# Layer 1 of a Perceiver kernel: memories loaded as layer 0 turned them, instead of turned a second time

## The chip, the cores and the metric

The kernel runs on one core of a Trainium2 chip, in float32. The metric is the device time of one launch in microseconds (us). Before the change it is 1710.55 us, the median of three runs from 1708.24 to 1710.9.

## What is computed

Two layers work on a latent array x of 16 batches x 64 rows x 256. Both read the same context memory, ctx_1024, of 16 batches x 1601 rows x 256. Layer 0 has a cross-attention that keeps the 32 best scores of a row, a retention step and a block of attention and experts. Layer 1 has the cross-attention that this change is about, a random-feature step and a tree of small networks. The part that matters, cut from the reference:

```python
x = x + L0_xattn(layernorm(x), ctx_1024, 32, ...)      # q k v; scores; top 32; softmax; weigh
x = x + L0_attn(layernorm(x), ...)                     # retention
x = x + L0_ffn(layernorm(x), ...)                      # attention, then experts
x = x + L1_xattn(layernorm(x), ctx_1024, ctx_1024, ...)

def L1_xattn(q, k, v, norm_w, norm_b, ..., Wq, bq, Wk, bk, Wv, bv, Wo, bo):   # H = 16 heads of 16
    qn, kn, vn = (layernorm(t, norm_w, norm_b) for t in (q, k, v))
    Q, K, V = (qn @ Wq + bq, kn @ Wk + bk, vn @ Wv + bv)                      # split into heads
    A = softmax(Q K^T / 4)
    O = A V + Q
    return layernorm(O, norm1_w, norm1_b) @ Wo + bo + O
```

Here layernorm(t, w, b) is (t - mean) * rsqrt(var + eps) * w + b over the 256 columns. In layer 1 it is applied to every row of every memory, while layer 0 uses the memories as they are.

## The kernel before

A memory is a tile of 128 partitions x 13 chunks x 256: row c * 128 + p stands in chunk c of partition p, and chunk 12 has 65 rows. `load_mem` (L213) brings one with two DMAs on SyncE's queue, 1536 KB (L215) and 65 KB (L218). TensorE contracts over partitions, so both layers need a memory turned, with its 256 columns on the partitions: a tile mT of 128 x 2 x 1601.

The code is traced by a framework that places the waits. By default a planner orders each engine's instructions, by program order and by when it estimates that each can start. Inside a `tc.manual_schedule(engines=...)` block the engines named keep the order of the program. [...]

**Layer 0** (L225 to L394) takes the memories in 8 pairs. `turned_pair(k)` (L237) loads the pair (six memory buffers, so three pairs), turns it on TensorE (L248, 52 transposes) and copies the result from PSUM with ScalarE (L253) into two mT buffers. `scored_pair(k)` (L284) makes the scores from mT (L290), `choose` (L302) takes the 32 best of each row with VectorE (L312, L316, L322), and `gather(k - 2)` (L325) turns the weights (L333) and weighs the unturned memories (L346). The loop at L370 runs gather(k - 2) in steps between the 16 steps of turned_pair(k), then scores pair k. No engine is in written-out order here. A pair's memory buffers come free when its gather ends.

**Between the layers** stand retention, attention and experts (L515 to L896). Layer 1's weights w_x (`load_square`, L92, on GpSimd's queue) and its work on the first memories, traced at L899 to L910, are filled in there by the planner: three memories are loaded and normalised (`fetch`, L504), two are turned, and keys and values of memory 0 are made.

**Layer 1's loop** (L1096 to L1151) runs over 128 units: 16 batches b, 4 parts of the 1601 rows (PARTS: 512, 384, 384 and 321 rows), 2 halves oc of the columns (8 heads each). TensorE, VectorE and ScalarE are in written-out order. A unit u does, in this order: `score` (four matmuls groups, L981); a step of `keys` for batch b + 1 (L460, L468); for four groups of heads the maximum on VectorE (L995) and the exponential on ScalarE (L997), with a step of `keys` between; `turn_over` of the unit before (L1010, L1015, L1017); a step of `values` for batch b + 1 (L482, L490); in units 1 to 3 of a batch a step of `collect` for the batch before; in units 3 to 7 steps of `normalise`; a step of `turned_mem`; `weigh` of the unit before (L1029, L1036); a second step of `values`.

- `normalise` (L408, for memory b + 3): 13 times statistics of a chunk on VectorE (L415, L416); then the square root on ScalarE (L419), a reciprocal (L421), and 13 times the normalising of a chunk in place on GpSimd (L426). Four steps a unit, and what is left in unit 7.
- `turned_mem` (L432, for memory b + 2): 8 steps, each 3 or 4 transposes on TensorE (L439) and one ScalarE copy (L444) that also applies norm_w and norm_b.
- `collect` (L1041): joins the four parts of a batch. GpSimd computes wt (L1049) and tot (L1051) in unit 1, with an exponential on ScalarE between (L1050); VectorE makes parts (L1068) in units 2 and 3; GpSimd adds them up in unit 3 (L1076, L1080, L1084) and writes by_head to DRAM (L1085).

So memory b + 3 is loaded at the start of batch b, normalised during it, turned in the next batch, projected to keys and values in the one after, and scored in the one after that.

Of the kernel before, what the change touches and what calls it, by code (L numbers as in the profile page):

```python
# [9 lines left out]
F32 = mybir.dt.float32  # L10
# [8 lines left out]
B = 16  # L19
# [13 lines left out]
TURN_STEPS = ((3, 0), (3, 1), (1, 0), (1, 1), (2, 0), (2, 1), (0, 0), (0, 1))  # L33
# [32 lines left out]
def perceiver_kernel(  # L66
# [24 lines left out]

    def load_square(pool, src, n, name):  # L92
        t = pool.tile([P, n, 2, D], F32, name=name, tag=name)
        nc.gpsimd.dma_start(
            out=t.rearrange("p n c o -> p (n c) o"),
            in_=src.rearrange("(m p) o -> p m o", p=P),
        )
        return t
# [124 lines left out]


    with ExitStack() as ph:  # L225
# [11 lines left out]
        def turned_pair(k, mems, memTs):  # L237

            for h in range(2):
                mems.append(load_mem(memp, 2 * k + h))  # L240
                memTs.append(work.tile([P, 2, S], F32, name="mT", tag="mT"))
            for n0, n in SCH:
                for h in range(2):
                    for dc in range(2):
                        pt = ps_m.tile([P, 512], F32, name="pt", tag="mm")
                        for j in range((n + P - 1) // P):
                            c = n0 // P + j
                            nc.tensor.transpose(  # L248
                                pt[:, j * P : j * P + chunk(c)],
                                mems[h][0 : chunk(c), c, dc * P : (dc + 1) * P],  # L250
                                ident[0 : chunk(c), 0 : chunk(c)],
                            )
                        nc.scalar.copy(memTs[h][:, dc, n0 : n0 + n], pt[:, 0:n])  # L253
                        yield

        first_mems, first_memTs = [], []
        for _ in turned_pair(0, first_mems, first_memTs):
            pass
# [23 lines left out]
        UT = act.tile([P, 2, NT], F32, name="UT", tag="b")  # L282

# [85 lines left out]
        mems, memTs = first_mems, first_memTs  # L369
        for k in range(NB + 2):  # L370
            last = gather(k - 2, *chosen.pop(k - 2)) if k >= 2 else iter(())
            if k < NB:
                if k > 0:
                    for step, _ in enumerate(turned_pair(k, mems, memTs)):
                        next(last, None)
                        if step % 2:
                            next(last, None)
                sco = work.tile([P, S], F32, name="sco", tag="sco", bufs=1)
                for _ in scored_pair(k, memTs, sco):
                    pass  # L380
            for _ in last:
                pass
            if k < NB:
                chosen[k] = (mems, *choose(sco))
                mems, memTs = [], []
# [14 lines left out]
    wp = x1.enter_context(tc.tile_pool(name="x1_w", bufs=1))  # L400
    memp = x1.enter_context(tc.tile_pool(name="x1_mem", bufs=2))
# [3 lines left out]
    w_x = load_square(wp, w_x1, 4, "w_x")  # L405
    wq, wk, wv, wo = (w_x[:, i, :, :] for i in range(4))

    def normalise(mt):  # L408

        st = small.tile([P, NC, 6], F32, name="m_st", tag="m_st")  # L410
        mv = small.tile([P, NC, 2], F32, name="m_mv", tag="m_mv")
        nc.gpsimd.memset(mv[:, 12, :], 1.0)
        for c in range(NC):
            m = chunk(c)
            nc.vector.bn_stats(out=st[0:m, c, :], in_=mt[0:m, c, :])  # L415
            nc.vector.bn_aggr(out=mv[0:m, c, :], in_=st[0:m, c, :])  # L416
            yield
        sd = small.tile([P, NC], F32, name="m_sd", tag="m_sd")
        nc.scalar.activation(sd, mv[:, :, 1], AF.Sqrt, bias=eps)  # L419
        rstd = small.tile([P, NC], F32, name="m_rstd", tag="m_rstd")  # L420
        nc.vector.reciprocal(rstd, sd)  # L421
        nmean = small.tile([P, NC], F32, name="m_nmean", tag="m_nmean")
        nc.gpsimd.tensor_scalar(nmean, mv[:, :, 0], -1.0, None, ALU.mult)
        for c in range(NC):
            m = chunk(c)
            nc.gpsimd.tensor_scalar(  # L426
                mt[0:m, c, :], mt[0:m, c, :], nmean[0:m, c : c + 1], rstd[0:m, c : c + 1],
                ALU.add, ALU.mult,
            )
            yield  # L430

    def turned_mem(mt, mT, pool):  # L432

        for part, dc in TURN_STEPS:
            c0, nch, n = PARTS[part]
            pt = pool.tile([P, 512], F32, name="pt", tag="mm")
            for j in range(nch):
                c = c0 + j
                nc.tensor.transpose(  # L439
                    pt[:, j * P : j * P + chunk(c)],  # L440
                    mt[0 : chunk(c), c, dc * P : (dc + 1) * P],
                    ident[0 : chunk(c), 0 : chunk(c)],
                )
            nc.scalar.activation(  # L444
                mT[:, dc, c0 * P : c0 * P + n], pt[:, 0:n], AF.Identity,
                bias=col("L1_norm_b", dc), scale=col("L1_norm_w", dc),
            )
            yield
# [4 lines left out]
    def keys(mT, kT, pool):  # L453

        for part, oc in KEY_STEPS:
# [3 lines left out]
            for dc in range(2):  # L459
# [9 lines left out]
                kT[:, oc, n0 : n0 + n], ps[:, 0:n], AF.Identity, bias=col("L1_bk", oc)  # L469
# [32 lines left out]
    mems, mTs, kvs, kvs_of = {}, {}, {}, {}  # L502

    def fetch(b):  # L504
        mems[b] = load_mem(memp, b)
        return normalise(mems[b])

    def run(steps):
        for _ in steps:
            pass  # L510
# [4 lines left out]
    with ExitStack() as ph:  # L515
# [69 lines left out]
        for k in range(NB):  # L585
            ps = ps_m.tile([P, D], F32, name="ps_o", tag="mm")
            nc.tensor.matmul(ps, lhsT=sT[:, k, :], rhs=v[:, k, :], start=True, stop=True)
            nc.vector.tensor_tensor(X[:, k, :], X[:, k, :], ps, ALU.add)

# [309 lines left out]
    for b in range(2):  # L899
        run(fetch(b))  # L900
    for b in range(2):
        mTs[b] = new_mT()
        run(turned_mem(mems.pop(b), mTs[b], ps_early))
        if b == 0:
            kvs[0] = new_kv(0)
            mT = mTs.pop(0)
            run(keys(mT, kvs[0][0], ps_early))
            run(values(mT, kvs[0][1], ps_early, nc.scalar.copy))
            run(fetch(2))
    early.close()  # L910

    with x1 as ph:
# [50 lines left out]

        bqv = act.tile([P, D], F32, name="bqv")
        nc.gpsimd.tensor_tensor(bqv, row("L1_bq"), row("L1_bv"), ALU.add)
# [132 lines left out]
        joining = made_k = made_v = turns = norms = iter(())  # L1098
        a = None
        order = {mybir.EngineType.PE, mybir.EngineType.DVE, mybir.EngineType.Activation}  # L1100
        with tc.manual_schedule(engines=order):
            for u in range(len(units) + 1):
                now = units[u] if u < len(units) else None
                if now is not None and now[1:] == (0, 0):
# [10 lines left out]
                    if b + 2 < B:  # L1115
                        mTs[b + 2] = new_mT()
                        turns = turned_mem(mems.pop(b + 2), mTs[b + 2], ps_m)
                    if b + 3 < B:
                        norms = fetch(b + 3)
# [16 lines left out]
                if u % 8 >= 3:  # L1136
                    for _ in range(4):
                        next(norms, None)
                if u % 8 == 7:
                    run(norms)  # L1140
                next(turns, None)
# [353 lines left out]
```

## Time and profile before

| what | us |
|---|---|
| median of three runs | 1710.55 |
| the profiled execution | 1709.81 |
| its span, first to last instruction | 1708.1 |
| TensorE busy | 1512.6 |
| VectorE busy | 1021.2 |
| ScalarE busy | 814.6 |
| GpSimd busy | 212.0 |

The profile is one execution. "Busy" is the time in which an engine computes; PE is TensorE, PEld its weight loads, DVE VectorE, ACT ScalarE, POOL GpSimd, SP SyncE (which only issues DMAs). The dearest groups of instructions that the change takes out, adds to or moves, as the profile lists them:

```profile
L426 POOL TENSOR_SCALAR memt<-memt,m_nmean,m_rstd 128x256 f32<-128x256 f32 x192 | 103.6, 557 | 7.3 <-PE po L1029 4.3 <-DVE m_rstd L421 2.9
...
L439 PE MATMUL pt<-ident,memt 128*128 128x128 f32 x384 | 65.1, 276 | 5.2 <-ACT aT L1015 3.3 <-ACT mT L444 1.6 <-ACT v L490 0.2
...
L444 ACT ACTIVATE mT<-pt,cols 128x384 f32<-128x384 f32 x64 | 42.7, 672 | 57.8 <-PE pt L439 57.6
```

A row reads: line, engine, operation, tile written and tiles read, shapes, count; then busy us in all and mean ns of one; then how long the engine stood idle just before such instructions and what ended that. The 276 ns of a transpose are its passage through the pipeline; back to back they follow each other faster.

### The profile page before, as it was taken

Reading aid. Unit: us, or ns where it says so; the run is one execution under the profiler, and the core shown is the slowest. Engines: PE = TensorE matmul, PEld = TensorE weight load, DVE = VectorE, ACT = ScalarE, POOL = GpSimd, SP = SyncE. Lnnn points to the kernel's source line nnn. Section 1 sums busy time; section 2 is a strip of 40 time slices with the busy share of each in tenths; the row PEclk is TensorE's granted clock in tenths of the full one; section 3 lists DMA queues with packets and bytes.
Section 4 is the critical chain, followed back from the end, with each engine's and each line's share of the span. In section 5 each row is a group of like instructions: output and inputs, shape, how many; then the busy total and the mean of one; then the engine's idle time right before and its main releaser. Section 6 shows DMA issues by size and latency. Waiting matters only on the chain.

```text
span 1708.1 us, 27877 instructions
## 1 busy us (share of the span) xinstructions
PE 1512.6 (89%) x10992; PEld 1008.2 (59%) x10992; DVE 1021.2 (60%) x2197; ACT 814.6 (48%) x1984; POOL 212.0 (12%) x405
## 2 busy tenths in 40 slices
PE   4899979992939999999999999999999973889997
PEld 3555546672836666666666666666667652544455
DVE  2667847771145777677767776777766665333122
ACT  3455531350005766666667666766666551212121
POOL 0000004201010120222021202120210001000000
PEclk9999989995969999999999999999999996889999
DMA  9044203223910101110011101110100003100000
GB/s 316 1 154 138 94 19 108 83 91 97 287 58 1 40 3 41 40 41 15 29 40 41 34 11 41 40 41 3 41 2 3 3 3 122 66 1 0 0 0 25
DMA packets 76034, 92.84 MB, mean 54 GB/s; under 512 B 2408, under 2 KB 71072, under 8 KB 75776
## 3 DMA queue, kind: packets, MB, share of 16 engines
q1 hardware_dynamic: 72064, 80.85, 14.9%
q0 software_dynamic: 2688, 9.17, 1.9%
q8 instruction: 86, 1.41, 0.4%
q10 hardware_dynamic: 1152, 1.05, 0.2%
q14 instruction: 44, 0.36, 0.1%
HBM read 85.82 MB, written 5.24 MB: 53 GB/s over the span
## 4 chain that ended last, share of the span: by engine, by line
PE 72%; ACT 10%; DVE 9%; issue 4%; DMA 3%; SPq 1%; POOL 0%; ACTq 0%; DVEq 0%; POOLq 0%
PE ps_v L482 10%; PE ps_k L460 7%; ACT a L997 6%; PE sc L981 6%; PE po L1029 6%; PE pt L1010 5%; PE ps_h L1334 5%; PE ps_p L183 3%; PE ps_o L1352 3%; PE pt L248 3%; PE sc L290 3%; PE pu L346 3%; PE pt L439 2%; PE ps_n L197 2%; DVE nmax L995 2%
## 5 line engine op out<-in xcount | busy, mean ns | idle before, releaser
L997 ACT ACTIVATE a<-sc,nmax 128x384 f32<-128x384 f32 (+2 forms) x512 | 300.3, 596 | 170.8 <-DVE nmax L995 170.5
L995 DVE TENSOR_REDUCE nmax<-sc 128x1 f32<-128x384 f32 (+2 forms) x512 | 258.2, 567 | 109.8 <-PE sc L981 109.7
L482 PE MATMUL ps_v<-w_x,mT 128*128 128x256 f32 (+1 forms) x832 | 205.3, 385 | 22.3 <-ACT kT L468 22.3
L1010 PEld LDWEIGHTS pt<-ident,a 128*128 128x128 f32 (+1 forms) x1664 | 189.3, 141 | 52.1 <-issue 28.2
L1017 DVE COPY aT<-pt 128x512 f32<-128x512 f32 (+1 forms) x288 | 191.0, 685 | 37.8 <-PE pt L1010 30.8
L1010 PE MATMUL pt<-ident,a 128*128 128x128 f32 (+1 forms) x1664 | 207.5, 274 | 2.3 <-ACT kT L468 0.7
L460 PE MATMUL ps_k<-mT,w_x 128*128 128x384 f32 (+2 forms) x512 | 207.9, 528 | 0.1
L482 PEld LDWEIGHTS ps_v<-w_x,mT 128*128 128x128 f32 (+1 forms) x832 | 144.7, 186 | 49.6 <-ACT kT L468 31.3
L460 PEld LDWEIGHTS ps_k<-mT,w_x 128*128 128x128 f32 x512 | 87.4, 190 | 108.1 <-issue 77.6
L1029 PE MATMUL po<-aT,v 128*32 128x128 f32 (+1 forms) x3328 | 119.1, 277 | 10.9 <-DVE aT L1017 7.0
L444 ACT ACTIVATE mT<-pt,cols 128x384 f32<-128x384 f32 (+2 forms) x128 | 87.1, 684 | 79.0 <-PE pt L439 76.3
L981 PE MATMUL sc<-kT,qh 32*128 32x384 f32 (+2 forms) x1024 | 123.1, 548 | 0.0
L426 POOL TENSOR_SCALAR memt<-memt,m_nmean,m_rstd 128x256 f32<-128x256 f32 (+1 forms) x208 | 112.2, 557 | 7.3 <-PE po L1029 4.3
L997 ACT ACTIVATION_READ_ACCUMULATOR a<-sc,nmax 128x1 f32 x512 | 105.1, 205 | 0.0
L1029 PEld LDWEIGHTS po<-aT,v 128*32 128x32 f32 (+1 forms) x3328 | 82.7, 109 | 35.5 <-issue 13.5
L490 DVE COPY v<-ps_v 128x512 f32<-128x512 f32 (+1 forms) x120 | 69.2, 576 | 49.3 <-PE po L1029 30.7
L415 DVE BATCH_NORM_STATS2 m_st<-memt 128x6 f32<-128x256 f32 (+1 forms) x208 | 82.6, 401 | 3.4 <-DMA memt<-in_mem_dram 3.0
L1334 PE MATMUL ps_h<-xnT,fw 128*128 128x512 f32 x192 | 84.1, 596 | 0.0
L253 ACT COPY mT<-pt 128x512 f32<-128x512 f32 (+1 forms) x128 | 58.0, 503 | 53.3 <-PE pt L248 52.6
L248 PE MATMUL pt<-ident,memt 128*128 128x128 f32 (+1 forms) x416 | 63.2, 292 | 22.8 <-DMA memt<-in_mem_dram 21.6
L468 ACT ACTIVATE kT<-ps_k,cols 128x384 f32<-128x384 f32 (+2 forms) x128 | 76.0, 593 | 13.2 <-PE ps_k L460 13.2
L1015 ACT COPY aT<-pt 128x512 f32<-128x512 f32 x128 | 76.9, 601 | 0.7 <-PE pt L1010 0.7
(310 smaller groups left out, 1945.8 us busy)
## 6 DMA issues: line engine op xcount, KB each, us to landing
memt<-in_mem_dram SPq DMA_DIRECT2D x32, 1536.0 KB, 9.1
w<-in_moe_w_dram SPq DMA_DIRECT2D x16, 1024.0 KB, 5.1
fw<-in_fff_w_dram SPq DMA_DIRECT2D x6, 1024.0 KB, 12.8
memt<-in_mem_dram SPq DMA_DIRECT2D x32, 65.0 KB
w_x<-in_w_x_dram POOLq DMA_DIRECT2D x2, 1024.0 KB, 12.2
rows<-in_rows_dram POOLq DMA_DIRECT2D x1, 1430.5 KB, 9.9
X<-in_x_dram SPq DMA_DIRECT2D x1, 1024.0 KB
w_mha<-in_w_mha_dram POOLq DMA_DIRECT2D x1, 1024.0 KB
```

Source lines behind the costliest of these rows:

```text
L248: nc.tensor.transpose(pt[:, j * P : j * P + chunk(c)], mems[h][0 : chunk(c), c, dc * P : (dc + 1) * P], ident[0 : chunk(c), 0 : chunk(c)],)
L426: nc.gpsimd.tensor_scalar(mt[0:m, c, :], mt[0:m, c, :], nmean[0:m, c : c + 1], rstd[0:m, c : c + 1], ALU.add, ALU.mult,)
L444: nc.scalar.activation(mT[:, dc, c0 * P : c0 * P + n], pt[:, 0:n], AF.Identity, bias=col("L1_norm_b", dc), scale=col("L1_norm_w", dc),)
L460: nc.tensor.matmul(ps[:, 0:n], lhsT=wk[:, dc, oc * P : (oc + 1) * P], rhs=mT[:, dc, n0 : n0 + n], start=(dc == 0), stop=(dc == 1),)
L482: nc.tensor.matmul(ps[0 : chunk(c), j, :], lhsT=mT[:, dc, c * P : c * P + chunk(c)], rhs=wv[:, dc, :], start=(dc == 0), stop=(dc == 1),)
L981: nc.tensor.matmul(scs[j][:, 0:n], lhsT=qh[rs, oc, b, :, :], rhs=kT[rs, oc, c0 * P : c0 * P + n], start=True, stop=True,)
L995: nc.vector.reduce_max(out=nm, in_=sc[:, 0:n], axis=AX.X, negate=True)
L997: nc.scalar.activation(aj[:, 0:n], sc[:, 0:n], AF.Exp, bias=nm, accum_out=tot[:, blk, part : part + 1])
L1010: nc.tensor.transpose(pt[0:m, j * P : (j + 1) * P], a[j][:, c * P : c * P + m], ident)
L1017: nc.vector.tensor_copy(aT[0:m, :], pt[0:m, :])
L1029: nc.tensor.matmul(po[32 * j : 32 * j + 32, :], lhsT=v[0:m, c0 + c, blk * 32 : (blk + 1) * 32], rhs=aTs[c][0:m, j * P : (j + 1) * P], star ...
L1334: nc.tensor.matmul(ps, lhsT=fw1[:, f, dc, m * P : (m + 1) * P], rhs=xnT[:, dc, cs], start=(dc == 0), stop=(dc == 1),)
```

## The change

Layer 0 already turns every memory. The change writes each turned memory to DRAM as layer 0 makes it, and layer 1 loads it from there instead of turning the memory again. A turned memory can't be normalised chunk by chunk with a per-partition factor, since a row's factor now runs along the free axis, so the norm is taken apart:

- rstd of each row is computed from the same statistics by `deviations`, with GpSimd alone instead of ScalarE's Sqrt and VectorE's reciprocal: a guess from the bits and four Newton steps, 18 small operations. It is written to DRAM (1664 values of 4 bytes). For memories 0 to 2 this happens in layer 0, from the loaded pairs; for memory b + 3 in batch b of layer 1's loop, from a fresh load of the memory.
- `scaled_mem` loads rstd broadcast to 128 partitions (rb, 820 KB) and the turned memory (mT, 1640 KB), and GpSimd multiplies mT by rb, in 8 products.
- mean, norm_w and norm_b go into the weights, once: wk and wv are scaled by norm_w and their column means are taken off, and norm_b becomes a bias of the keys (kbias) and part of bqv, which is added with the query's bias at the end.

In layer 0 SyncE keeps the order of the program: the loads of the first three pairs, then each pair's 8 stores (one after the second copy of each of 4 stretches x 2 memories) and the load of the next pair at the end of an iteration, after the gather. Before, that load was traced at the start of the next iteration. In layer 1's loop GpSimd and SyncE join the engines in program order. Weight loads go through SyncE instead of GpSimd.

```diff
     def load_square(pool, src, n, name):
-        nc.gpsimd.dma_start(
+        nc.sync.dma_start(
...
+    def deviations(b, mt):
+        st = small.tile([P, NC, 6], F32, name="m_st", tag="m_st")
+        mv = small.tile([P, NC, 2], F32, name="m_mv", tag="m_mv")
+        nc.gpsimd.memset(mv[:, 12, :], 1.0)
+        for c in range(NC):
+            m = chunk(c)
+            nc.vector.bn_stats(out=st[0:m, c, :], in_=mt[0:m, c, :])
+            nc.vector.bn_aggr(out=mv[0:m, c, :], in_=st[0:m, c, :])
+            yield
+        var = small.tile([P, NC], F32, name="m_var", tag="m_var")
+        nc.gpsimd.tensor_scalar(var, mv[:, :, 1], EPS, None, ALU.add)
+        rs = small.tile([P, NC], F32, name="m_rs", tag="m_rs")
+        bits = rs.bitcast(I32)
+        nc.gpsimd.tensor_scalar(
+            bits, var.bitcast(I32), -0.5, float(0x5F3759DF), ALU.mult, ALU.add
+        )
+        sq = small.tile([P, NC], F32, name="m_sq", tag="m_sq")
+        for _ in range(4):
+            nc.gpsimd.tensor_tensor(sq, rs, rs, ALU.mult)
+            nc.gpsimd.tensor_tensor(sq, sq, var, ALU.mult)
+            nc.gpsimd.tensor_scalar(sq, sq, -0.5, 1.5, ALU.mult, ALU.add)
+            nc.gpsimd.tensor_tensor(rs, rs, sq, ALU.mult)
+        nc.gpsimd.dma_start(out=rstd_d[b].rearrange("(c p) -> p c", p=P), in_=rs)
+        yield
...
         def turned_pair(k, mems, memTs):
             for h in range(2):
-                mems.append(load_mem(memp, 2 * k + h))
...
                         nc.scalar.copy(memTs[h][:, dc, n0 : n0 + n], pt[:, 0:n])
+                        if dc == 1:
+                            nc.sync.dma_start(
+                                out=turned_d[2 * k + h][:, :, n0 : n0 + n],
+                                in_=memTs[h][:, :, n0 : n0 + n],
+                            )
                         yield
...
+        in_order.enter_context(tc.manual_schedule(engines={mybir.EngineType.SP}))
+        loaded = {k: load_pair(k) for k in range(3)}
...
+        for b in range(3):
+            run(deviations(b, loaded[b // 2][b % 2]))
...
             for _ in last:
                 pass
+            if 2 <= k < NB - 1:
+                loaded[k + 1] = load_pair(k + 1)
...
-    memp = x1.enter_context(tc.tile_pool(name="x1_mem", bufs=2))
+    memp = x1.enter_context(tc.tile_pool(name="x1_mem", bufs=1))
...
+    def scaled_mem(b, mT):
+        rb = memp.tile([P, S], F32, name="rb", tag="rb", bufs=2)
+        nc.sync.dma_start(out=rb, in_=rstd_d[b][0:S].partition_broadcast(P))
+        nc.sync.dma_start(out=mT, in_=turned_d[b])
+        yield
+        for c0, _, n in PARTS:
+            for dc in range(2):
+                sl = slice(c0 * P, c0 * P + n)
+                nc.gpsimd.tensor_tensor(mT[:, dc, sl], mT[:, dc, sl], rb[:, sl], ALU.mult)
+                yield
...
+    for wi in (wk, wv):
+        for c in range(2):
+            nc.gpsimd.tensor_scalar(wi[:, c, :], wi[:, c, :], col("L1_norm_w", c), None, ALU.mult)
+        ps = ps_early.tile([P, D], F32, name="ps_wm", tag="mm")
+        for c in range(2):
+            nc.tensor.matmul(ps, lhsT=mean, rhs=wi[:, c, :], start=(c == 0), stop=(c == 1))
+        for c in range(2):
+            nc.vector.tensor_tensor(wi[:, c, :], wi[:, c, :], ps, ALU.subtract)
...
-        order = {mybir.EngineType.PE, mybir.EngineType.DVE, mybir.EngineType.Activation}
+        order = {
+            mybir.EngineType.PE, mybir.EngineType.DVE, mybir.EngineType.Activation,
+            mybir.EngineType.Pool, mybir.EngineType.SP,
+        }
...
                     if b + 2 < B:
                         mTs[b + 2] = new_mT()
-                        turns = turned_mem(mems.pop(b + 2), mTs[b + 2], ps_m)
+                        scaling = scaled_mem(b + 2, mTs[b + 2])
+                        next(scaling)
                     if b + 3 < B:
-                        norms = fetch(b + 3)
+                        norms = deviations(b + 3, load_mem(memp, b + 3))
...
                 if u % 8 >= 3:
-                    for _ in range(4):
+                    for _ in range(3):
                         next(norms, None)
-                if u % 8 == 7:
-                    run(norms)
-                next(turns, None)
+                if u % 8 in (3, 4, 5, 6):
+                    for _ in range(2):
+                        next(scaling, None)
```

`normalise`, `turned_mem` and `fetch` are gone. The biases kbias and bqv are made the same way as the folded weights, with six small matmuls.

## The prediction, made before the changed kernel was run

> **What bounds the kernel now.** I read the page's engine shares and its chain first, to learn which engine sets the end; then the busy windows cut at layer 1's batches, because the change touches that loop most; then the timeline inside one batch and inside one pair of layer 0.
>
> ```profile
> PE 1512.6 (89%) x10992; PEld 1008.2 (59%) x10992; DVE 1021.2 (60%) x2197; ACT 814.6 (48%) x1984; POOL 212.0 (12%) x405
> ...
> PE 72%; ACT 10%; DVE 9%; issue 4%; DMA 3%; SPq 1%; POOL 0%; ACTq 0%; DVEq 0%; POOLq 0%
> ```
>
> TensorE carries the chain; GpSimd and SyncE are almost absent from it. In the loop of layer 1 every batch has the same period. The first vector maximum (L995) of batches 12, 13, 14 and 15 starts at 1203.15, 1259.32, 1313.35 and 1364.48, so these windows are whole batches:
>
> ```profile
> core 0: us, PE busy (x) PEld busy (x) DVE busy (x) ACT busy (x) POOL busy (x), PEclk, DMA share, GB/s
> 1203.15:1259.32 56.17, 53.87 (x495) 37.88 (x495) 41.02 (x93) 37.60 (x100) 10.99 (x21) 1.00 0.10 30
> 1259.32:1313.35 54.03, 53.32 (x495) 37.84 (x495) 35.01 (x67) 35.17 (x97) 3.71 (x7) 1.00 0.02 3
> 1313.35:1364.48 51.13, 50.41 (x469) 34.69 (x470) 35.00 (x66) 29.69 (x89) 3.72 (x7) 1.00 0.02 3
> ```
>
> This is an experiment the kernel makes on itself. Batch 12 turns a memory and normalises another; batch 13 only turns (no memory 16 to normalise); batch 14 does neither, but still keys, values, scores and collect. Turning costs 54.03 - 51.13 = 2.90 us; normalising 56.17 - 54.03 = 2.14. Of the latter 1.67 falls in units 3 and 4 (15.11 us together against 13.44 in batch 13, from the starts of L995), the rest in unit 7, where Sqrt changes ScalarE's table (L419 and back at L997, 1.28 us each). Why unit 3:
>
> ```profile
> 1004.12 0.86 DVE L1068 TENSOR_TENSOR parts<-pt,wt 64x256 f32<-64x256 f32 x2 [1.41 <-PE pt L1062]
> 1005.01 0.43 DVE L415 BATCH_NORM_STATS2 m_st<-memt 128x6 f32<-128x256 f32 x1
> ...
> 1007.25 0.69 DVE L490 COPY v<-ps_v 128x512 f32<-128x512 f32 x1
> 1007.86 1.94 DVE L995 TENSOR_REDUCE nmax<-sc 128x1 f32<-128x384 f32 x4
> ```
>
> Four statistics steps (1005.01 to 1007.25, 2.24 us) stand ahead of the next unit's maxima. Layer 0 has a period too:
>
> ```profile
> 114.67:138.04 23.37, 22.67 (x153) 12.67 (x151) 17.18 (x16) 12.62 (x26) 0.00 (x0) 1.00 0.45 141
> ```
>
> ```profile
> 114.87 0.37 SPq L215 DMA_DIRECT2D memt<-in_mem_dram  x1
> ...
> 116.18 0.37 SPq L215 DMA_DIRECT2D memt<-in_mem_dram  x1
> ```
>
> ```profile
> 120.92 0.45 ACT L253 COPY mT<-pt 128x65 f32<-128x65 f32 x3 [0.48 <-PE pt L248]
> ```
>
> ```profile
> 123.03 0.55 PE L248 MATMUL pt<-ident,memt 128*128 128x128 f32 x3
> ...
> 128.45 0.66 PE L248 MATMUL pt<-ident,memt 128*128 128x128 f32 x4
> ```
>
> A pair's two memories are asked for at 114.87 and 116.18 and land 7.4 and 10.9 us later (DMA view of those stretches), at 122.3 and 127.1; their first transposes are at 123.03 and 128.45. Only about 1 us of cover is left, and TensorE is 97% busy.
>
> **What the Trainium skill says.** "GPSIMD Engine Reference", section 3.1: a two-input elementwise operation costs GpSimd about 2.6 cycles an element, twice VectorE. The trace agrees: 727 ns for 256 elements (L1076), 2.1 ns per further one. "DMA: Bandwidth & Descriptors", section on issuing engines: all queues share the same 16 engines, so moving weight loads to SyncE saves issue time only; no row here contradicts it. The same page, rules for authors: a strided last dimension gives one descriptor per element; this bears on the rstd write (4-byte pieces), and no run here shows one. The nearest row, by_head with 64-byte pieces, lands in 2.7 us.
>
> **Part by part. The loop.** Gone per batch: 26 transposes (L439), 8 evictions (L444, 0.68 us), Sqrt, 13 POOL steps (L426, 557 ns). That is batch 14, 51.13 us, plus what stays of normalising: 13 statistics steps, three a unit in units 3 to 6 and one in unit 7. Unit 3: three take 2.24 x 3/4 = 1.69; four cost 1.67, so 0.57 was slack; without the turning the next scores come 0.33 earlier (batch 13 against 14), leaving 0.24, so the loss is 1.45. Units 4 to 6 hold it: VectorE would be 5.7 us busy in 6.1 to 6.5 long units; I add 0.1. Steady batch: 51.13 + 1.55 = 52.7, or 3.5 less. Batches 1 to 12: 12 x 3.5 = 42; batch 0, without a collect, 2.90 + 0.68 for Sqrt, say 3.4; batch 13: 2.9; 14 and 15 nothing. **Loop: -48.**
>
> Added there. GpSimd: eight products, 1.27 + 1.0 + 1.0 + 0.86 us twice = 8.3; 18 small steps at 0.25 (L1051, L1049) = 4.5; the rstd DMA at 0.9 to 1.4 (L1085: 879 ns). With collect's 3.7 that is 17 to 18 us of 52. Its written order holds collect's steps behind the chain of unit 7, which ends about 3 us into the next batch; collect's first (wt) is due in unit 1, at 6.6.
> SyncE: rb waits for rstd's landing; mT and memt are queued behind it. Statistics step 13 ends some 4 us into unit 7, the chain 4.6 later, the DMA about 3.5 later: 6.5 us into the next batch. One memory takes 8.0 from issue to landing here, 4.6 of it data at 345 GB/s (the layer 0 stretch); before it now 0.82 + 1.64 MB, 6.1 to 7.1 us. So memt lands at about 6.5 + 0.4 + 14.5 = 21, and is due at unit 3's first statistics step, 20 + 5.9 = 26. Cover 4.5 us: cost nothing. Lower bound 0, since a hidden load cannot gain; the upper bound is the slower rival. The products need mT at 20 and rb by then; both landed.
>
> **Layer 0.** 26 MB of stores join: 64 DMAs, eight a pair, each waiting for its ACT copy. A pair moves 6.6 MB, 19 us of 23.4 at 345 GB/s. What moves is the order: load_pair(k+1) stands behind the last store of pair k. Its copy ends at 121.4, two stores at 0.4 each: loads at 122.2 instead of 114.87, 7.3 us late, landing at 129.6 and 134. Affected are pairs 3 to 7 (0 to 2 are loaded ahead). If TensorE takes the whole gather of the pair before (13 + 52 matmuls, about 10 us) into that gap, 1 to 2 us a pair is left: 7 in all. If its order stays, 7.3 less 1 to 1.4 of cover, 6 a pair: 30. The planner fills by estimated readiness, so in part: **+15.** The reuse of the mT buffers now waits for stores too; these land before the loads, so I cost that at nothing; without that cover it would add to the same 7.3. Statistics of memories 0 to 2 (39 steps of 0.5 us) go to VectorE between 24 and 58, where it is nearly idle waiting for TensorE: nothing. Weight loads on SyncE ahead of the memories: the same bytes before memory 1, landing 23.5: nothing, at most 1 either way.
>
> **Between the layers.** Turning memories 0 and 1 stood in the chain at 295 to 302 and 373 to 379: about 3 us gone. Folding the norm into wk and wv adds 10 matmuls (1.7 us), 6 VectorE and 8 GpSimd steps, and may make TensorE wait in order for w_x, asked for at 260.7 in the page's run: 0 to 6. **Sum 0, bounds -4 and +6.**
>
> The profiled execution took 1709.81 (span 1708.1 and 1.7 around it), the median 1710.55, 0.04% above. 1709.8 - 48 + 15 + 0 = 1677.
>
> **Rivals.** Likeliest (0.52): loop -46 to -50, layer 0 +8 to +25, between -4 to +6: 1664 to 1692, point 1677.
> Layer 0 hidden (0.15): gathers fill the gap wholly. For: 10 us of gather are ready at 119. Against: program order interleaves it with the transposes. 1709.8 - 48 + 7 - 4 = 1665, or down to 1657.
> Layer 0 keeps its order (0.15): 30 there, 6 between. For: the order of 123.03 to 128.45; against: a planner that knows the loads are late. 1709.8 - 48 + 30 + 6 = 1698, up to 1710.
> Slower (0.18): the rstd write. 1664 pieces of 4 bytes are 104 on each of 16 engines; if each takes 0.13 us, it lands some 13 us later than by_head's 2.7; memt then comes 8.5 us after unit 3 wants it, VectorE stops in order, and with it the maxima and TensorE: 12 batches x 8.5 = 102, 1779. It decides from 4.5 us of lateness on and outweighs the gain from 4.5 + 33/12 = 7.3. Against: by_head's 64 pieces an engine land in 2.7 us in all.
>
> **The numbers.** Differences under 0.2% (3.4 us) cannot be told from none here. Same: 0.03, from the upper end of the third case and mild lateness in the fourth. Faster: 0.52 + 0.15 + 0.13 = 0.80. Slower: 0.17. The range 1656 to 1708 holds the first three cases but for their ends.
>
> **What would show it.** Right: batches of 52 to 53 us, unit 3 near 8.1, no L439-like transposes, no Sqrt table loads in the loop, statistics not waiting for a DMA. Layer 0: pairs 3 to 7 longer than 23.4, by 1 to 6, idle TensorE before transposes put down to memt. Wrong: statistics waiting for memt, or products for mT; a pair above 30 us; TensorE waiting for w_x near 265.

## The result: 3.7% slower

| | before | after |
| --- | --- | --- |
| median of four runs | 1709.55 | 1773.76 |
| range | 1708.24 to 1710.9 | 1771.63 to 1774.47 |
| ratio (95% interval) | 1 | 1.037 (1.0355 to 1.0391) |
| span of the profiled execution | 1708.1 | 1772.6 |
| loop of layer 1 in it, first maximum to last | 869.3 | 879.9 |
| layer 0, to the last gather | 245.6 | 294.1 |
| between layer 0 and the loop | 288.5 | 298.4 |
| behind the loop | 304.7 | 300.3 |

The forecast was 1677, and the range ended at 1708. Here is the profile after the change, in the order in which the one before was read: first the page, with its engine shares, the chain that ended last by engine, and two rows of the costliest groups.

```profile
PE 1508.3 (85%) x10596; PEld 995.4 (56%) x10596; DVE 1023.1 (58%) x2187; ACT 696.3 (39%) x1814; POOL 307.6 (17%) x615
...
PE 62%; DMA 16%; DVE 9%; ACT 6%; issue 4%; SPq 2%; POOL 2%; ACTq 0%; DVEq 0%; POOLq 0%
...
L282 PE MATMUL pt<-ident,memt 128*128 128x128 f32 (+1 forms) x416 | 69.0, 313 | 70.4 <-DMA memt<-in_mem_dram 53.7
L235 DVE BATCH_NORM_STATS2 m_st<-memt 128x6 f32<-128x256 f32 (+1 forms) x208 | 83.4, 402 | 46.7 <-DMA memt<-in_mem_dram 46.7
```

TensorE has 396 matmuls fewer, yet is only 4.3 us less busy, and DMAs went from 3% to 16% of the chain. Two groups stand still until a memory lands: the turning in layer 0 (53.7 us, of which 20.9 are the wait for the first two memories, which was there before the change too) and the statistics (46.7 us, of which 38.5 lie in the loop). Next come the busy windows of batches 12 to 14, cut at the first maxima (L1035 now):

```profile
1274.06:1331.27 57.21, 53.67 (x469) 36.42 (x469) 40.85 (x93) 29.53 (x89) 16.81 (x36) 0.94 0.23 74
1331.27:1382.19 50.92, 50.46 (x469) 34.72 (x469) 34.86 (x67) 29.54 (x89) 15.76 (x30) 1.00 0.16 51
1382.19:1433.11 50.92, 50.46 (x469) 34.73 (x470) 34.92 (x67) 29.53 (x89) 3.71 (x7) 1.00 0.02 3
```

Batch 13 still scales a memory on GpSimd (15.76 us busy) and takes exactly as long as batch 14, which doesn't. What replaced the turning, loads of turned memories and products on GpSimd, costs nothing on the path there. Batch 12, which also takes statistics of a new memory, is 1.04 us longer than before; batches 1 to 12 take 57.6 on average. Three timelines inside batch 4, which starts at 809.47, tell why. They are those of GpSimd, SyncE and VectorE, and between the first two stands a row of the waits of SyncE's queue:

```profile
814.26 1.24 POOL L252 DMA_DIRECT2D rstd<-m_rs  x1 [0.87 <-POOL m_rs L251]
```

```profile
SPq L462 <- DMA rstd<-m_rs: 601.7, 12, 54.0
```

```profile
824.08 0.33 SPq L462 DMA_DIRECT2D rb<-rstd  x1
824.50 0.38 SPq L463 DMA_DIRECT2D mT<-turned  x1
824.99 0.38 SPq L219 DMA_DIRECT2D memt<-in_mem_dram  x1
```

```profile
834.06 0.86 DVE L1108 TENSOR_TENSOR parts<-pt,wt 64x256 f32<-64x256 f32 x2 [1.41 <-PE pt L1102]
838.97 0.43 DVE L235 BATCH_NORM_STATS2 m_st<-memt 128x6 f32<-128x256 f32 x1 [4.05 <-DMA memt<-in_mem_dram]
```

The write of the row factors (rstd) is issued at 814.26. SyncE's rb waits for it until 824.08, which is 9.8 us (9.1 to 10.2 in batches 1 to 13), and since SyncE takes its list in order, mT and memt, queued behind rb, leave only 0.4 and 0.9 us after it. (The row of waits gives 601.7 us for twelve, because SyncE stands at this instruction for most of a batch.) VectorE is ready for the statistics at 834.9 and gets the memory 4.05 us later. Unit 3 takes 12.21 us and unit 4 8.08. The two units have different causes. Batches 2 and 6 both wait 2.38 us for the memory, and unit 3 takes 10.55 and 10.54 us in them. The windows of their unit 4, first of batch 2, then of batch 6, have the granted TensorE clock in the third column from the end:

```profile
728.06:734.12 6.06, 4.32 (x45) 2.85 (x45) 5.21 (x14) 3.57 (x11) 6.06 (x7) 1.00 0.01 1
956.26:964.82 8.56, 6.82 (x45) 4.38 (x45) 5.33 (x14) 3.57 (x11) 7.50 (x8) 0.60 0.06 6
```

The same 45 matmuls take 2.5 us longer where the clock is 0.60. So the wait lengthens unit 3, and the clock, which falls behind the wait in 11 of batches 1 to 12, lengthens unit 4. Against the 8.19 and 6.06 us of e1_mem_first below, unit 3 loses 38 us over these batches and unit 4 loses 24. In the windows of the write, in batch 4, the last two columns are the DMA engines' busy share and GB/s:

```profile
814.00:818.00 4.00, 4.00 (x46) 2.52 (x45) 2.58 (x5) 1.37 (x4) 1.24 (x1) 1.00 0.21 6
818.00:824.00 6.00, 5.62 (x62) 3.79 (x61) 4.26 (x10) 3.83 (x13) 0.48 (x2) 1.00 0.00 0
828.00:832.00 4.00, 4.00 (x34) 2.72 (x27) 3.23 (x8) 2.53 (x9) 0.00 (x0) 1.00 1.02 401
```

From 818 to 824 no DMA engine moves anything: SyncE waits for a write of 6.5 KB whose packets are recorded as over by 817.4. What fills the rest of the time is not shown. In layer 0 a pair (here from one choice to the next) takes 30.47 us where it took 23.37:

```profile
145.32:175.79 30.47, 24.49 (x151) 15.09 (x151) 17.31 (x16) 13.03 (x25) 0.00 (x0) 0.89 0.66 213
```

SyncE's and ScalarE's timelines give the cause, and TensorE's gives the price:

```profile
139.14 1.66 SPq L289 DMA_DIRECT2D turned<-mT  x2
140.90 0.57 SPq L219 DMA_DIRECT2D memt<-in_mem_dram  x1
```

```profile
138.90 0.45 ACT L287 COPY mT<-pt 128x65 f32<-128x65 f32 x3 [0.49 <-PE pt L282]
```

```profile
149.64 1.11 PE L282 MATMUL pt<-ident,memt 128*128 128x128 f32 x4 [5.98 <-DMA memt<-in_mem_dram]
```

The loads follow the pair's last copy and last stores, and TensorE then has nothing to do for 6 us. The clock of this pair is 0.89, where it was 1.00 before, so the rest of the loss may be the clock; that was not separated here. Pair 1 has another wait: in ScalarE's timeline the copies into the mT buffers begin at 73.30 only, when pair 0's stores have left these buffers.

```profile
73.30 1.56 ACT L287 COPY mT<-pt 128x512 f32<-128x512 f32 x3 [10.38 <-DMA turned<-mT]
```

Its period is 31.7 instead of 15.6; that of pair 2 is 23.1 instead of 27.3, so the two together lose 11.9. In all: layer 0 +48.4, the loop +10.5, between them +9.9, behind the loop -4.4, which is the 64.5 of the spans.

### The profile page after: what moved, and what is told of

It is laid out like the page before. It is cut to its first block, busy times and chain, and to the rows that moved or that the text cites. A ratio compares the mean times of both kernels' runs of the same rounds, so it can differ in the third digit from the quotient of the medians.

```text
span 1772.6 us, 27389 instructions
## 1 busy us (share of the span) xinstructions
PE 1508.3 (85%) x10596; PEld 995.4 (56%) x10596; DVE 1023.1 (58%) x2187; ACT 696.3 (39%) x1814; POOL 307.6 (17%) x615
## 4 chain that ended last, share of the span: by engine, by line
PE 62%; DMA 16%; DVE 9%; ACT 6%; issue 4%; SPq 2%; POOL 2%; ACTq 0%; DVEq 0%; POOLq 0%
DMA memt<-in_mem_dram 12%; PE ps_v L503 9%; PE ps_k L481 6%; PE pt L1050 5%; PE po L1069 5%; PE sc L1021 5%; PE ps_h L1378 5%; ACT a L1037 4%; PE ps_o L1396 3%; PE pt L282 3%; PE pu L393 3%; PE ps_p L187 2%; PE ps_n L201 2%; DVE nmax L1035 2%; PE ps_h L905 2%
## 5 line engine op out<-in xcount | busy, mean ns | idle before, releaser
L1035 DVE TENSOR_REDUCE nmax<-sc 128x1 f32<-128x384 f32 (+2 forms) x512 | 258.4, 567 | 99.9 <-PE sc L1021 91.1
L1050 PE MATMUL pt<-ident,a 128*128 128x128 f32 (+1 forms) x1664 | 213.6, 278 | 32.8 <-DVE v L511 30.6
L503 PE MATMUL ps_v<-w_x,mT 128*128 128x256 f32 (+1 forms) x832 | 223.2, 410 | 17.1 <-ACT kT L489 17.1
L503 PEld LDWEIGHTS ps_v<-w_x,mT 128*128 128x128 f32 (+1 forms) x832 | 156.6, 200 | 46.2 <-ACT kT L489 23.9
L468 POOL TENSOR_TENSOR mT<-mT,rb 128x384 f32<-128x384 f32 (+2 forms) x128 | 127.7, 1032 | 60.9 <-DMA mT<-turned 55.1
L1069 PE MATMUL po<-aT,v 128*32 128x128 f32 (+1 forms) x3328 | 124.0, 284 | 12.9 <-ACT aT L1055 6.7
L282 PE MATMUL pt<-ident,memt 128*128 128x128 f32 (+1 forms) x416 | 69.0, 313 | 70.4 <-DMA memt<-in_mem_dram 53.7
L235 DVE BATCH_NORM_STATS2 m_st<-memt 128x6 f32<-128x256 f32 (+1 forms) x208 | 83.4, 402 | 46.7 <-DMA memt<-in_mem_dram 46.7
L1076 ACT COPY pos<-po 128x128 f32<-128x128 f32 x128 | 33.9, 265 | 188.9 <-PE po L1069 188.9
L282 PEld LDWEIGHTS pt<-ident,memt 128*128 128x128 f32 (+1 forms) x416 | 54.9, 162 | 90.1 <-DMA memt<-in_mem_dram 36.7
L489 ACT ACTIVATE kT<-ps_k,kbias 128x384 f32<-128x384 f32 (+2 forms) x128 | 76.0, 593 | 27.7 <-PE ps_k L481 27.7
```

The costliest lines, as they stand in the source:

```text
L282: nc.tensor.transpose(pt[:, j * P : j * P + chunk(c)], mems[h][0 : chunk(c), c, dc * P : (dc + 1) * P], ident[0 : chunk(c), 0 : chunk(c)],)
L468: nc.gpsimd.tensor_tensor(mT[:, dc, sl], mT[:, dc, sl], rb[:, sl], ALU.mult)
L503: nc.tensor.matmul(ps[0 : chunk(c), j, :], lhsT=mT[:, dc, c * P : c * P + chunk(c)], rhs=wv[:, dc, :], start=(dc == 0), stop=(dc == 1),)
L1035: nc.vector.reduce_max(out=nm, in_=sc[:, 0:n], axis=AX.X, negate=True)
L1050: nc.tensor.transpose(pt[0:m, j * P : (j + 1) * P], a[j][:, c * P : c * P + m], ident)
L1069: nc.tensor.matmul(po[32 * j : 32 * j + 32, :], lhsT=v[0:m, c0 + c, blk * 32 : (blk + 1) * 32], rhs=aTs[c][0:m, j * P : (j + 1) * P], star ...
```

## Experiments

All are edits of the changed kernel, and ratios are to the kernel before the change.

### The loop: order of the queue, or size of the pieces?

e1_mem_first puts the memory's load ahead of what waits for the row factors:

```diff
+                    if b + 3 < B:
+                        norms = deviations(b + 3, load_mem(memp, b + 3))
                     if b + 2 < B:
...
                         next(scaling)
-                    if b + 3 < B:
-                        norms = deviations(b + 3, load_mem(memp, b + 3))
```

> Edit: in the loop the load of the memory of b+3 stands ahead of rb and mT of b+2 in SyncE's order; nothing else changes. Theory Q (the loss of each batch is SyncE's queue: rb waits for a rstd write that lands about 10 us after its issue, and memt stands behind rb): memt no longer waits, DVE's 4 us wait on memt in unit 3 goes, batches 1 to 12 come out at about 52.5 instead of 57 to 58, the loop about 60 shorter, total about 1714; rb and mT still go out late but well before the next batch. Rival T (the late memt is a DMA system slowed by the 4-byte writes, wherever memt stands): memt still lands late, batches stay at 56 to 58, total within 15 of 1774. Both: layer 0 as after (294 us to the last gather).

Measured: 1713.24 (ratio 1.0019, 1.0012 to 1.0026), 60.5 less. Batches 1 to 12 are 52.5 on average, unit 3 takes 8.19 and unit 4 6.06, and the clock of these batches is 1.00. SyncE's timeline for the same batch (start 795.02), then GpSimd's:

```profile
793.36 0.38 SPq L219 DMA_DIRECT2D memt<-in_mem_dram  x1
793.79 0.81 SPq L222 DMA_DIRECT2D memt<-in_mem_dram  x1
809.70 0.33 SPq L462 DMA_DIRECT2D rb<-rstd  x1
810.12 0.38 SPq L463 DMA_DIRECT2D mT<-turned  x1
```

```profile
799.83 1.24 POOL L252 DMA_DIRECT2D rstd<-m_rs  x1 [0.87 <-POOL m_rs L251]
```

The write is as late as before, 9.9 us from its issue to rb, and it costs nothing now, since only mT, not wanted until unit 3, stands behind it. e2_rstd_52B leaves the order and makes the pieces fewer and longer:

```diff
-        nc.gpsimd.dma_start(out=rstd_d[b].rearrange("(c p) -> p c", p=P), in_=rs)
+        nc.gpsimd.dma_start(out=rstd_d[b].rearrange("(p c) -> p c", p=P), in_=rs)
```

> Changes the computation: the row factors of each memory are written in a permuted order, 128 pieces of 52 bytes instead of 1664 of 4 bytes, so that rows are scaled by other rows' factors; times are read only. Theory S (the size of the pieces makes the write land late and slows what runs beside it): the write lands about 2.7 us after its issue as by_head does, batches 1 to 12 about 52.7, the wait of 16.3 us ahead of pair 1 in layer 0 is gone, total about 1697 (-60 in the loop, -16 in layer 0). Rival (pieces of this count or the Newton chain ahead of it make it late, not their size): rstd still lands about 10 us after issue, total within 10 of 1774.

Measured: 1701.1 (0.9944, 0.9928 to 0.9961), 72.7 less; batches 1 to 12 are 52.4. In batch 4 (start 786.09):

```profile
790.33 0.64 POOL L252 DMA_DIRECT2D rstd<-m_rs  x1 [0.29 <-POOL m_rs L251]
```

```profile
793.79 0.33 SPq L462 DMA_DIRECT2D rb<-rstd  x1
```

Now rb goes out 3.5 us behind the write's issue here, and 1.8 in most other batches, and the memory is in time in the old order. Either edit alone removes the loop's whole loss. The two conditions had to meet: a late write, and a memory queued behind its reader. Whether the number of pieces or their size makes the write late is open, as the edit changes both. In layer 0 the period of pair 1, the first, shrank to 20.2 too, so the writes have a part in that stall.

### Layer 0: the loads behind the stores

e3_load_early issues the next pair's loads ahead of the last four stores:

```diff
                         if step % 2:
                             next(last, None)
+                        if step == 8 and 2 <= k < NB - 1:
+                            loaded[k + 1] = load_pair(k + 1)
...
-            if 2 <= k < NB - 1:
-                loaded[k + 1] = load_pair(k + 1)
```

(A pair has 16 steps, and the loads follow the ninth; the expectation counts them wrongly.)

> Edit: in layer 0 the loads of pair k+1 go out after the eighth of pair k's twelve steps, ahead of the stores of its last four, instead of behind them all. Theory B (the 7 us that each of pairs 3 to 7 lost are the loads standing behind the last stores on SyncE): periods of pairs 3 to 7 drop from 30.6 to between 23.4 and 28, total 15 to 36 less, 1738 to 1759. Rival (the stores' own traffic, or the mT buffers that wait for them, hold the pair at 30): periods stay at 30 to 31, total within 8 of 1774. Loop as after in both.

Measured: 1745.01 (1.0208, 1.0174 to 1.0243), 28.8 less. Pairs 3 to 7 take 23.5, 25.7, 24.9, 24.9 and 25.8. So four fifths of the 38.3 us that they had lost came from the place of the load in the queue. e3_store_pool takes the stores off that queue instead:

```diff
-                            nc.sync.dma_start(
+                            nc.gpsimd.dma_start(
                                 out=turned_d[2 * k + h][:, :, n0 : n0 + n],
```

> Edit: layer 0's stores of the turned memories are issued by GpSimd instead of SyncE, so that the loads do not stand behind them on a queue. Theory B (order on SyncE's queue): periods of pairs 3 to 7 go back from 30.6 to 23.4 to 24.5, total about 36 less, 1738; the wait ahead of pair 1 stays at about 16. Rival (traffic of the stores, 3.2 MB for each pair beside loads of as much): periods stay at 30 to 31. A third outcome is that GpSimd's gathers of the pair stand behind the waiting stores: periods then go above 31, total over 1774.

Measured: 1763.37 (1.0322, 1.029 to 1.0354), only 10.4 less; pairs 3 to 7 take 28.6 to 31. Pair 1 went to 15.6, but pair 2 to 37.4: the wait for the buffers moved by one pair. In the waits of SyncE's queue the loads now stand still for TensorE's gather, which frees a memory buffer, and TensorE's timeline shows the other half of the circle:

```profile
SPq L219 <- PE pu L393: 131.6, 5, 55.9
```

```profile
178.09 1.09 PE L282 MATMUL pt<-ident,memt 128*128 128x128 f32 x4 [4.12 <-DMA memt<-in_mem_dram]
```

The second memory's load, issued at 160.5, lands at 178. The loads of this pair go out 9.9 us ahead of the next choice, as early as before the change, but a free queue alone doesn't bring the memory in time. The page "DMA: Bandwidth & Descriptors" of the Trainium skill, section "Issuing engines are not separate DMA queues", says that DMAs of all issuing engines run on the same 16 engines and interleave. This run agrees, with 17.6 us for a load that took 10.9 beside loads alone. Asking for the load before the stores was worth more.

### Layer 0: the wait of pair 1

e4_defer moves the three writes of layer 0 to the end of the text of layer 0, still on GpSimd:

```diff
-        nc.gpsimd.dma_start(out=rstd_d[b].rearrange("(c p) -> p c", p=P), in_=rs)
+        if b < 3:
+            nc.gpsimd.tensor_copy(kept_rs[:, b, :], rs)
+        else:
+            nc.gpsimd.dma_start(out=rstd_d[b].rearrange("(c p) -> p c", p=P), in_=rs)
...
+        for b in range(3):
+            nc.gpsimd.dma_start(
+                out=rstd_d[b].rearrange("(c p) -> p c", p=P), in_=kept_rs[:, b, :]
+            )
```

> Edit: the three rstd writes of layer 0 (4-byte pieces) go out after its last pair instead of during pairs 0 and 1; the statistics and the chain stay where they are. Theory S (these writes slow the stores of pair 0, for which ScalarE's mT copies of pair 1 wait): the first period of layer 0 falls from 29 to 32 to between 15.6 (as before the change) and 20 (as with the 52-byte pieces), total 9 to 16 less, 1758 to 1765. Rival (the stores of pair 0 are late because they share the DMA engines with the loads of five memories, whatever the writes do): first period stays at 29 or more, total within 4 of 1774. Pairs 2 to 7 and the loop as after in both.

Measured: 1778.6 (1.0394, 1.0378 to 1.041), first period 29.0. It decides nothing: GpSimd isn't in written-out order there, and the planner issued the writes at 32.6, 43.3 and 50.4, where they had been; why it is 4.8 us slower than the changed kernel is open. e9_sp_defer does it on SyncE, inside its written order:

```diff
+        for b in range(3):
+            nc.sync.dma_start(
+                out=rstd_d[b].rearrange("(c p) -> p c", p=P), in_=kept_rs[:, b, :]
+            )
         in_order.close()
```

> Edit: the row factors of memories 0 to 2 are kept on the chip and written by SyncE, in its written-out order, behind the stores of layer 0's last pair, in the same 4-byte pieces. (In e4_defer the writes stood later in the text only: GpSimd's order is the planner's there, and it issued them at 32.6, 43.3 and 50.4 us as before.) Theory S (these writes slow the stores of pair 0, for which ScalarE's copies of pair 1 wait): first period of layer 0 falls from 29 to 32 to about 20, as with the 52-byte pieces, pairs 2 to 7 stay, total about 1762 (-9 to -12), provided the three writes at the end meet nothing that waits. Rival: first period stays at 29 or more, total within 4 of 1774.

Measured: 1766.84 (1.0329, 1.0313 to 1.0345), 6.9 less; first period 19.9, copies no longer waiting for a store. The windows of 35 to 45, of the changed kernel and then of this one:

```profile
35.00:40.00 5.00, 5.00 (x13) 2.28 (x12) 5.00 (x27) 2.06 (x3) 3.65 (x16) 1.00 1.44 208
40.00:45.00 5.00, 5.00 (x13) 2.17 (x12) 3.14 (x10) 1.27 (x2) 4.40 (x5) 1.00 0.98 59
```

```profile
35.00:40.00 5.00, 5.00 (x13) 2.14 (x12) 5.00 (x27) 2.06 (x3) 3.41 (x16) 1.00 1.11 340
40.00:45.00 5.00, 5.00 (x13) 2.28 (x12) 3.39 (x10) 1.27 (x2) 4.35 (x9) 1.00 1.07 367
```

With the 4-byte write issued at 31.9 on its way beside loads and stores, the engines are busy (0.98) but move 59 GB/s; without it, 367. Pair 1 still takes 4.3 us longer than before the change, but pair 2 takes 4.2 less, 23.1 instead of 27.3: pairs 1 and 2 together are back at 43.0 against 42.8, so nothing of their loss is left. (ScalarE copied four times ahead of the exponential before, and now doesn't.)

### Together

e6_three takes e1, e3_load_early and the edit of e4_defer; e10_all the edit of e9_sp_defer in place of the last; e11_mT3 adds `bufs=3` to layer 0's mT tile.

> Three edits together: memory ahead of rb and mT in the loop, layer 0's loads after the eighth step, layer 0's rstd writes after its last pair. If the losses are separate, they add: -60, -29 and -9 to -16, so 1669 to 1676, ratio to before 0.976 to 0.980. If one hides another (a queue freed in one place meeting the next limit), the total lies above 1690.

> Memory ahead of rb and mT in the loop, layer 0's loads after the eighth step, and the three row-factor writes on SyncE behind the last pair. If the losses are separate: the 1680 of e6_three less 9 to 12, 1668 to 1672, ratio to before 0.975 to 0.977. If the writes, moved, delay the weights of the next stage that SyncE issues behind them: 1676 to 1684.

> As e10_all with three mT buffers in layer 0 instead of two. If the 1.5 us that pairs 3 to 7 still lose to the kernel before, and the 4.6 of pair 1, are waits for the turned stores to free an mT buffer: up to 7 + 5 less than e10_all, 1657 to 1668. Rival (they are the order of TensorE, which the planner made another): within 2 of e10_all.

Measured: e6_three 1680.58 (0.9829, 0.9816 to 0.9842), where e4_defer's edit does nothing; the other two sum to 1773.8 - 60.5 - 28.8 = 1684.5, within 4 us of it. e10_all 1671.05 (0.9772, 0.9751 to 0.9793). e11_mT3 1666.84 (0.9746, 0.9733 to 0.9759), with pair 3 at 23.3 and pairs 4 to 7 at 24.1, so the third buffer is worth 5.6 us over the five pairs; pair 1 still takes 19.4. The losses of loop, loads and writes are separate and add. The page of e11_mT3:

```profile
PE 1467.3 (88%) x10596; PEld 964.2 (58%) x10596; DVE 1020.8 (61%) x2187; ACT 693.0 (42%) x1814; POOL 304.7 (18%) x615
...
PE 72%; ACT 10%; DVE 10%; DMA 4%; issue 3%; SPq 1%; POOL 0%; ACTq 0%; DVEq 0%; POOLq 0%
```

The chain has nearly the shares that it had before the change. TensorE is 45 us less busy, and its mean granted clock is 0.952, where it was 0.954 before the change and 0.921 in the changed kernel. The number of matmuls is that of the changed kernel, so a slower clock fits the 41 us that these took longer there.

### Between the layers

e8_fold is e6_three with the folding of the norm (L604 to L634) traced ahead of retention:

> As e6_three, and the folding of the norm into wk and wv is traced ahead of retention instead of behind it, so that GpSimd scales the weights ahead of batch 0's products. Theory F (the fold after retention, with GpSimd's scaling behind the products, put 5 us between retention and attention): 2 to 5 less than e6_three. Rival (it only moves, and delays retention by the same work on TensorE and VectorE): within 1 of e6_three.

Measured: 1680.97, against 1680.58. Retention ends 5.2 us later, and attention starts 0.3 us sooner: the fold takes its 5 us wherever it stands.

The other loss there is at the expert gate. TensorE's timeline of the changed kernel:

```profile
428.48 1.66 PE L169 MATMUL ps_t<-ident,y 128*128 128x128 f32 x8 [2.27 <-DVE y L774]
432.59 0.69 PE L169 MATMUL ps_t<-ident,y 128*128 128x128 f32 x2 [2.46 <-DVE y L774]
...
434.67 6.41 PE L826 MATMUL ps_g<-wg,y1T 128*128 128x8 f32 x30
```

Thirty gate products take 6.41 us; before the change the same thirty took 3.52. The windows around them, before and then after, have the granted clock in the third column from the end:

```profile
378.00:383.00 5.00, 4.95 (x44) 4.69 (x42) 2.08 (x5) 3.24 (x4) 0.00 (x0) 1.00 1.06 389
```

```profile
431.00:432.00 1.00, 0.00 (x0) 0.00 (x0) 1.00 (x4) 0.24 (x1) 0.00 (x0) 0.75 1.05 369
432.00:441.00 9.00, 8.41 (x40) 8.40 (x40) 3.01 (x7) 1.87 (x2) 0.00 (x0) 0.50 0.79 294
```

Where TensorE now idles, it had been turning memory 1. e12_fill puts work there that nobody needs:

```diff
+            if k < 4:
+                ps = ps_m.tile([P, 512], F32, name="ps_fill", tag="mm")
+                for j in range(6):
+                    nc.tensor.transpose(ps[:, 0:P], y1[:, k, 0:P], ident)
```

> As e11_mT3, with 24 added transposes of y1's first four chunks on TensorE, whose results nobody reads, in the stretch before the gate where TensorE now waits for VectorE for 2.3 and 2.5 us. Before the change layer 1's transposes of a memory stood there, and the 32 gate products took 3.5 us at a granted clock of 1.00; after it they take 6.4 at 0.50. Theory C (the idle stretch lowers the clock that TensorE is granted): the gate products take about 3.5 again, total 2 to 3 less than e11_mT3, 1664. Rival (something else lowers it): they take 6.4, total as e11_mT3 or up to 1 more.

Measured: 1664.97 (0.9729, 0.9716 to 0.9743), 1.9 less than e11_mT3. Its timeline and its window have:

```profile
388.38 4.09 PE L839 MATMUL ps_g<-wg,y1T 128*128 128x8 f32 x30 [0.17 <-DVE y1T L138]
```

```profile
387.00:393.00 6.00, 5.31 (x39) 4.59 (x37) 2.40 (x6) 1.87 (x2) 0.00 (x0) 0.84 1.06 371
```

The intervals of the two totals overlap, so the total shows little. But the same products take 4.09 us instead of 6.41, and work in the idle stretch was all that was added: the idling had halved the clock ahead of them. That is half of the account. In this run too the clock falls, at 391.1, in the midst of these products, which then follow each other after 0.21 us instead of 0.11; that is why they don't come down to 3.52. TensorE had not been idle for more than 0.4 us since 382.5, so idling just before the fall is not its reason here, and the reason is not shown. The page "TensorE: Matmul & The Clock Gate" of the Trainium skill, Part 1, says that TensorE falls to half rate after an idle window of about 3.4 us. In the changed kernel it fell at 431.5, by the window of 431 to 432, after a gap of 2.3 us, 1.7 us of work and 1.4 us of a second gap, so less idling was enough.

## Why the prediction was wrong

The forecast was 97 us too low: 58 of them in the loop (+10.5 instead of -48), 33 in layer 0 (+48.4 instead of +15), 10 between the layers, and 4 less behind the loop.

**The work removed and added: right.** Batches of 52.7 were predicted, and 52.4 to 52.5 came out in e1_mem_first and e2_rstd_52B; unit 3 at 8.1 against 8.19; batches 13 and 14 at 51.13 against 50.92. GpSimd's products took 8.2 us a batch against 8.3. The loop of e1_mem_first is 819.7, 49.6 less than before the change, against the 48 predicted.

**The step that failed in the loop** is "the DMA about 3.5 later: 6.5 us into the next batch". The write landed 9.8 after its issue, not 3.5, and was issued 4.8 into the batch, not 3.0; so rb went out at 14.6. What followed was priced well: memt landed 14.9 us later, as worked out, and was due at 25.5 against 26. The cover of 4.5 less the 8.1 of lateness is -3.6, and VectorE waited 4.05. The wait is 3.2 us on average over batches 1 to 12. The lower clock behind it, for which the prediction has no term, adds 2.0, and with both a batch is 5.1 us longer than in e1_mem_first, 61 in all. The nearest row was the wrong neighbour: by_head has 64-byte pieces, and the page "DMA: Bandwidth & Descriptors" of the Trainium skill, "Rules for kernel authors", had warned that a strided last dimension gives one descriptor for each element, here of 4 bytes. The fourth rival had the place, the chain of waits and the point of decision. Its price supposed that the pieces take long to move, while the windows show them moved by 818 and nothing moving until 824. That its total of 1779 comes near the 1774 measured is luck: its loop is about 43 us too slow, and layer 0 and the stretch between, which it leaves at the point forecast, hide that.

**Layer 0: the upper bound was the answer.** "The planner fills by estimated readiness, so in part" stood for +15. This is the step that failed in layer 0. The order stayed, pairs 3 to 7 took 30.5 to 32.7, and that is 38 us, more than the rival's 30: the pair shown turns its first memory 8.7 us after the load's issue, where it landed in 7.4. e3_load_early returned 30 of it by moving the load ahead in the queue.

**A cost put at nothing that wasn't.** For the reuse of the mT buffers the prediction said that the stores "land before the loads". In pairs 3 to 7 TensorE did wait for the loads; with these moved ahead, a third buffer was worth about 1 us a pair. For pair 1, whose memories were loaded beforehand, no load covers the stores. It lost 16.1, of which pair 2 gave 4.2 back, and 11.8 of it goes when the 4-byte writes go elsewhere (19.9 for 31.7; 9 against the 29.0 of other runs with the same order there).

**Between the layers** -4 to +6 was given, and +9.9 came (7 to 10 in the later profiles with the fold and the gate as they are): about 5 for the fold, near its upper bound, and 2.9 for a TensorE clock for which the prediction has no term. For the 2 us that are left, and for the 4.4 gained behind the loop, nothing was tried.

## What to carry to other kernels

Before a load is put on a queue in written-out order, look at what stands ahead of it: a reader that waits for someone's write holds back every prefetch behind it, and putting the prefetch first cost nothing here and was worth 60 us. Don't price a small strided write by its bytes: measure one in pieces of the same size, alone and beside other traffic. When stores join a stage whose loads have little time to spare, ask for the loads before the last stores of the stage, and count buffers for both. When a wait stops TensorE, look at the granted clock behind it: the price can be more than the wait.

## What the hardware showed that was not expected

- A write of 1664 pieces of 4 bytes to DRAM landed 9.1 to 10.2 us after its issue in the loop, in the batch shown with all DMA engines idle for the last 6; the same bytes in 128 pieces of 52 landed in 1.8 to 3.5. Beside other traffic it brought the DMA engines from 367 to 59 GB/s for 5 us at nearly the same busy share.
- A wait can cost more after it has ended: with the same wait of 2.38 us in two batches, the unit behind it took 6.06 us at a granted clock of 1.00 and 8.56 at 0.60.
- Removing TensorE's filler work made later TensorE work slower: at a granted clock of 0.50 instead of 1.00, thirty products took 6.41 us instead of 3.52. With useless work put back they took 4.09, because the clock fell all the same, only later.
